# Two-layer cross-attention block: the feed-forward's short matmuls grouped by row shape, its neighbours taken two at a time, and the first group's keys made first

## The chip, the core and the metric

The kernel runs on one core of a Trainium2 chip. The metric is the time of one execution on the device, in microseconds (us), as the median of several runs. The kernel before takes 3205.06 us (3 runs, 3204.47 to 3205.57).

A core has a matmul engine (PE in the profile; its loading of the stationary operand is PEld), and three engines for elementwise work: VectorE (DVE), ScalarE (ACT) and GpSimd (POOL). SyncE (SP) issues most transfers. Each engine works through its own list of instructions in order; semaphores tie the lists together. Matmul results go to PSUM, 8 banks of 128 x 512 floats.

## What is computed

Two layers of the same block over `x` (4 x 512 x 320) with a context (4 x 1601 x 192): self-attention, cross-attention, feed-forward, all in float32. Cut to what matters here:

```python
def _attn(x, ctx, wq, wk, wv, wo, bo, heads):        # 20 heads of 16
    q, k, v = heads_of(x @ wq), heads_of(ctx @ wk), heads_of(ctx @ wv)
    a = softmax(einsum('bhid,bhjd->bhij', q, k) * 16 ** -0.5)
    return merged(einsum('bhij,bhjd->bhid', a, v)) @ wo + bo

h1 = _ln(x, n1_g, n1_b)
x = _attn(h1, h1, q1, k1, v1, o1_w, o1_b, heads) + x
h2 = _ln(x, n2_g, n2_b)
x = _attn(h2, context, q2, k2, v2, o2_w, o2_b, heads) + x
h3 = _ln(x, n3_g, n3_b)
proj = h3 @ ff_w1 + ff_b1                            # 320 -> 2560
a, g = split(proj, 2, axis=-1)
ff = a * gelu(g) @ ff_w2 + ff_b2                     # 1280 -> 320
return ff + x
```

## The kernel before

The work is a list of *units* in a fixed order. In each layer there are 20 units of self-attention (4 batch items, 5 groups of 4 heads), 20 of cross-attention and 4 of feed-forward (one for each batch item). `main` (L1065) runs an attention unit, `ff_main` (L1170) a feed-forward unit. The program is written out by hand in the order in which each engine is to work (a manual schedule), so what stands next to what on PE is decided while the kernel is built.

**Side work.** Everything that is not the core of a unit is put in *chains* of steps: layer norms (`turn`, L490: transposes into the tile `hps`, the matmuls of L497), query and key projections (`queries` L693 and `keys` L719: tiles `qps`, `kps`), values (`vps`), and the output projections after attention (`project` L1016: tile `ops`). The matmuls of the projections and of the values use 32 columns of the PE array at a time, four of them side by side; one step is 12 matmuls. A step has a cost (an estimate in the units of the planner, 0.95 for an output projection, 1.43 for queries or keys of self-attention) and a due round. `tick` adds to a credit in each round, enough for all steps to be done by when they are due, up to 4.0. `steps` (L398) takes steps off the chains as long as the credit allows: beside the feed-forward (`beside` true) a first step needs 0.5 of its cost in credit, and a second one right behind it 3.0 of its cost; `steps(False)` takes a step only at a credit of 3.0.

**Feed-forward.** The 320 rows of `ff_w1` are cut into two slices of 128 rows and a rest of 64 rows. The tile `w1r` holds the rest for the `a` half of the columns on partitions 0 to 63 and for the `g` half on partitions 64 to 127; `hT[:, 2]` holds the last 64 rows of the input twice, to match. A chunk `c` is 128 of the 1280 hidden columns; there are 10. For each chunk `full` (L1192) makes the four matmuls of 128 rows (two slices for `a`, two for `g`; L1194) and `rest` (L1203) the two of 64 rows, which use the two halves of the array at the same time (L1206). `gate` (L1210) then computes gelu on ACT and the product on DVE (L1213), which gives the tile `hid` (some chunks lie in the `kT` buffer). Chunks go in pairs. In float32 one matmul of the program is two in the profile: the eight matmuls of a pair's `full` are x16, its four of `rest` x8. After the ten chunks come four products with `ff_w2` (tile `yps`, L1233, 40 matmuls in all) and the addition to `x`. `beside` (L1173) is called before the first and before the second chunk of a pair and after each `yps`: it lets `give` put in rounds of the next attention unit's score maxima (tile `sps`, L903) and calls `steps`.

**PSUM.** `ps_st` has 4 tiles of one bank, `ps_m` 2 tiles of two banks. A pair of chunks takes two of the first kind for `a` and one of the second for `g`. A step beside the feed-forward takes a tile of `ps_st`, a round of maxima one of `ps_m` and two of `ps_st`. A tile is free again when its last reader (for `a` the product on DVE) is done.

**The start.** The first layer norm is followed by queries and keys of units 0 and 1; `to_slots` (L632) moves those of unit 0 out of PSUM in four pieces each, alternately on ACT and DVE (L643, L641). Then come four rounds of unit 0's score maxima (`sps`, reduced on DVE, L919), with a step of values between two rounds; `max_end` (L963) writes the maxima into the query tile by eight small transfers, two of them on POOL's queue, after which the first scores (`st`, L1074) may start. While `start["on"]` is set, steps take `ps_m` tiles once the rounds have begun.

Of the kernel before, what the change touches and what calls it, by code (L numbers as in the profile page):

```python
# [9 lines left out]
F32 = mybir.dt.float32  # L10
# [9 lines left out]
FF = 4 * D  # L20
L = 2
EPS = 1e-5
P = 128
# [20 lines left out]
NHC = FF // P  # L44
# [4 lines left out]
FK = [(0, 0, P), (1, P, P)]  # L49
REST = D - 2 * P  # L50
# [16 lines left out]
def kernel(ctx: ExitStack, tc: tile.TileContext, x, context, ws, out):  # L67
# [18 lines left out]
    nc = tc.nc  # L86
# [9 lines left out]
    ps_st = ctx.enter_context(tc.tile_pool(name="ps_st", bufs=4, space=PSUM))  # L96
    ps_m = ctx.enter_context(tc.tile_pool(name="ps_m", bufs=2, space=PSUM))
# [8 lines left out]
    for b in range(2):  # L106
        k, o = (const.tile([P, 1], F32, name=f"{n}{b}") for n in ("keep", "ones"))
# [11 lines left out]
    for i in range(2):  # L119
        m = const.tile([P, SLOT], F32, name=f"nmax{i}")  # L120
# [26 lines left out]
    for b in range(2):  # L147
        k = const.tile([P, 1], F32, name=f"kept{b}")
# [5 lines left out]
    for b in range(2):  # L154
        rows = slice(b * GD, (b + 1) * GD)
# [20 lines left out]
    w1 = wpool.tile([P, 2, 2 * FF], F32, name="w1")  # L176
# [6 lines left out]
    w1r = wpool.tile([P, FF], F32, name="w1r")  # L183
# [121 lines left out]
    at = 0  # L305
# [23 lines left out]
    chains = {n: deque() for n in ("divide", "project", "slots", "norm", "context", "early", "proj", "values")}  # L329
# [6 lines left out]
    start = {"on": True, "both": False}  # L336

    def step_bank(shape, name):

        if start["on"] and start["both"]:  # L340
            return ps_m.tile([P, 2, 512], F32, tag="m", name=name)[:, 0]
        return ps_st.tile(shape, F32, tag="st", name=name)

    def warm(n):

        ps = step_bank([P, 512], "wps")
        for _ in range(n):
            nc.tensor.matmul(ps[:, : 4 * P], lhsT=ident, rhs=fill, start=True, stop=True)
# [4 lines left out]
    def add(chain, cost, f, due, ready=yes, soon=yes):  # L353
        chains[chain].append((cost if isinstance(cost, tuple) else (cost,), due, ready, soon, f))
# [7 lines left out]
    def pick():  # L362
        heads = [
            (q[0][1] + late_by(n), n)
            for n, q in chains.items()
            if q and q[0][2]() and q[0][3]() and (q[0][0][0] != LIGHT or clock["lights"])
        ]
        return min(heads)[1] if heads else None

    def run(chain):  # L370
        costs, _, ready, _, f = chains[chain].popleft()
        assert ready(), chain
        f()
        clock["credit"] -= sum(costs)
# [19 lines left out]
    def tick():  # L394
        clock["round"] += 1
        clock["credit"] = max(-2.0, min(4.0, clock["credit"] + pace()))

    def steps(beside, lights=1):  # L398


        tick()
        clock["lights"], clock["slots"] = lights, 1
        clock["tiles"] = True if beside is None else None
        done = 0
        while True:
            name = pick()
            if name is None:
                break
            cost = sum(chains[name][0][0])
            if cost >= 0.1:  # L410
                share = (0.5, 3.0) if beside else (9.0, 9.0) if beside is False else (0.5, 0.75, 1.5)
                least = cost * share[done] if done < len(share) else 3.0
                if clock["credit"] < (3.0 if beside is False else least):
                    break
                done += 1
                if clock["tiles"] is not None:
                    clock["tiles"] = name in ALIKE
            run(name)
            if cost == LIGHT:
                clock["lights"] -= 1  # L420
            clock["slots"] -= name == "slots"
        clock["tiles"] = None

    def until(test, name):
        while not test():
            assert chains[name], name
            run(name)
# [221 lines left out]
    def add_proj(u):  # L649
        wq, wk = wq2 if u.cross else wq1, wk1  # L650
        chain = "early" if u.early else "proj"
# [13 lines left out]
        first = units[u.i - u.g]  # L665
# [125 lines left out]
        def add_queries():  # L791
            if u.g == 0 and u.cross:
                add(chain, 0.0, hold, due - 4, yes, lambda: "h" in u.own)
            for part in range(parts):
                add(chain, (0.05 + 0.427 / parts,) * 3, lambda part=part: queries(part), due - 2, unread)

        if not u.cross:
            add_queries()
            add(chain, (0.477,) * 3, keys, due, free)
        else:  # L800
            add(chain, 2.45, keys_of_context, keys_due, free)
            add_queries()
            for _ in range(HG):
                add(
                    "slots", 0.0, lambda: u.kslots and u.kslots.popleft()(), keys_due,
                    lambda: u.keyed, lambda: clock["slots"] > 0,
                )
# [251 lines left out]
    def round_of(scores, maxima):  # L1059

        then = [f() for f in scores] + [f() for f in maxima]
        for f in then:
            f()
# [106 lines left out]
    def ff_main(u, give, nxt):  # L1170
        done = 0

        def beside(room, n):  # L1173

            nonlocal done
            if room:
                for extra in give(done, True)[1]:
                    round_of([], extra)
            done += n
            if done == u.steps - 1 and nxt is not None and nxt.kind != "ff":  # L1180
                max_reduce(nxt)
                max_end(nxt)
            steps(True)
            for _ in range(n - 1):
                steps(False)

        hc = one.tile([P, 6, N], F32, tag="ctxT", name="hid")
        hid = [hc[:, i, :] for i in range(6)]

        hid += [kbuf[1][:, i * N : (i + 1) * N] for i in range(3)] + [kbuf[2][:, :N]]  # L1190

        def full(c, i, ps):  # L1192
            for k, at, n in FK:
                nc.tensor.matmul(  # L1194
                    ps,
                    lhsT=w1[:, k, i * FF + c * P : i * FF + (c + 1) * P],
                    rhs=u.hT[:, k, :],
                    start=(k == 0),
                    stop=False,
                )  # L1200
            return ps

        def rest(c, pss):  # L1203
            for i, ps in enumerate(pss):
                rows = slice(i * REST, (i + 1) * REST)
                nc.tensor.matmul(  # L1206
                    ps, lhsT=w1r[rows, c * P : (c + 1) * P], rhs=u.hT[rows, 2, :], start=False, stop=True
                )

        def gate(c, pss):  # L1210
            gl = prs.tile([P, N], F32, tag="pr", name="gl")
            nc.scalar.activation(gl, pss[1], AF.Gelu, bias=b1[:, NHC + c : NHC + c + 1])  # L1212
            nc.vector.scalar_tensor_tensor(hid[c], pss[0], b1[:, c : c + 1], gl, ALU.add, ALU.mult)  # L1213

        for c in range(0, NHC, 2):

            beside(True, 2)
            gates = ps_m.tile([P, 2, 512], F32, tag="m", name="fps")
            pss = []
            for i in range(2):  # L1220
                if i:
                    beside(False, 2)
                ps = ps_st.tile([P, 512], F32, tag="st", name="fps")
                pss.append([full(c + i, 0, ps), full(c + i, 1, gates[:, i])])
            for i in range(2):
                rest(c + i, pss[i])
            for i in range(2):
                gate(c + i, pss[i])
        ff_read.append(u)
        for t in range(NQ):  # L1230
            ps = ps_st.tile([P, 512], F32, tag="st", name="yps")
            for c in range(NHC):
                nc.tensor.matmul(  # L1233
                    ps[:, :D],
                    lhsT=hid[c][:, t * P : (t + 1) * P],
                    rhs=w2[:, c, :],
                    start=(c == 0),
                    stop=(c == NHC - 1),
                )
            nc.vector.tensor_tensor(xs[u.b][:, t, :], ps[:, :D], xs[u.b][:, t, :], ALU.add)  # L1240
            if u.l == L - 1:
                dma(out=out[u.b, t * P : (t + 1) * P, :], in_=xs[u.b][:, t, :])
            beside(True, 1)
        after(u)
# [35 lines left out]
    def left(v):  # L1280
        return sum(map(len, v.pairs))
# [75 lines left out]

    add_norms(0)
    add_proj(units[0])
    warm(5)  # L1360
    add_proj(units[1])
    until(lambda: not chains["proj"], "proj")
    add_values(units[0])
    add_proj(units[2])
    first = units[0]
    first.pairs = max_pairs(first)
    start["both"] = True
    while left(first):
        round_of([], first.pairs[0].popleft() + first.pairs[1].popleft())
        if left(first):  # L1370
            run("values")

    run("proj")
    run("values")
# [8 lines left out]
    start["on"] = start["both"] = False  # L1383
    run("proj")

    for _ in range(3):
        run("values")
    clock["credit"] = 0.0

# [45 lines left out]
```

## Time and profile before

| | us |
|---|---|
| median of 3 runs | 3205.06 |
| the profiled execution | 3204.68 |
| its span (first to last instruction) | 3202.9 |
| PE busy in the span | 3167.7 |
| DVE / ACT / POOL busy | 2068.9 / 1972.4 / 1202.3 |
| feed-forward of layer 0: 1329.77 to 1633.00 | 303.23, PE busy 299.75 |
| feed-forward of layer 1: 2920.14 to 3202.90 | 282.76, PE busy 278.68 |
| the first 36 us | PE busy 29.75 |

The profile page has a line of busy time for each engine and, further down, groups of equal instructions. The timeline view lists instructions in order of time, merged where equal ones follow each other: start, length, engine, line, operation, output<-inputs, rows*columns of the PE array that a matmul uses, its size and how many (x); in square brackets the idle time before it and what ended it. As matmuls are pipelined and their ends are modelled, lengths overlap; the time that a group takes is read from its start to the start of the next. "The granted clock" is the share of its full clock that PE was given.

### The profile page before, as it was taken

The page shows a single profiled execution, that of the slowest core. Times are in us where ns is not written, and L with a number is a line of the kernel's source. Part 1 is how long each engine was busy: PE and PEld are TensorE (multiplying, and loading weights), DVE is VectorE, ACT ScalarE, POOL GpSimd, SP SyncE. Part 2 cuts the span into 40 slices and gives each one's busy share as a digit, 9 for nine tenths or more (in the row PEclk, how much of TensorE's full clock was granted, in tenths as well). Part 3 has the DMA queues.
Part 4 walks back from the last instruction along what each step waited for, and adds up shares of the span by engine and source line. Part 5 has one row for each costly group of instructions (what it writes and reads, how often), then busy time and mean ns, then how long its engine had stood idle before and what let it go on. Part 6 is the DMA issues. An engine that isn't in the chain of part 4 may idle for free. (4 is left out here: it accounts for less than half of the span.)

```text
span 3202.9 us, 81370 instructions
## 1 busy us (share of the span) xinstructions
PE 3167.7 (99%) x33970; PEld 1462.6 (46%) x33970; DVE 2068.9 (65%) x2663; ACT 1972.4 (62%) x3951; POOL 1202.3 (38%) x1617
## 2 busy tenths in 40 slices
PE   8999999999999999999999999999999999999999
PEld 3444444444444444354444444444444444443555
DVE  7787778778678677422247777777777777773221
ACT  4666577777777777611146665778778777785110
POOL 5555334443443443201125553344444444432000
PEclk9999999999999999999999999999999999999999
DMA  2220011100100100100012100110010010001000
GB/s 66 56 70 17 14 27 38 33 21 20 32 21 21 31 16 11 39 6 0 1 30 61 34 14 14 24 27 16 16 32 9 16 32 11 14 10 37 9 11 15
DMA packets 104851, 77.84 MB, mean 24 GB/s; under 512 B 42908, under 2 KB 95012, under 8 KB 104484
## 3 DMA queue, kind: packets, MB, share of 16 engines
q1 hardware_dynamic: 104400, 72.63, 9.2%
q8 instruction: 268, 4.39, 0.6%
q14 instruction: 99, 0.81, 0.1%
q0 software_dynamic: 64, 0.00, 0.0%
q10 hardware_dynamic: 20, 0.00, 0.0%
HBM read 33.04 MB, written 7.93 MB: 13 GB/s over the span
## 5 line engine op out<-in xcount | busy, mean ns | idle before, releaser
L1080 ACT ACTIVATE pr<-st 128x512 f32<-128x512 f32 (+1 forms) x2720 | 1408.8, 602 | 430.1 <-PE sps L903 366.4
L1074 PE MATMUL st<-q,kT 32*128 32x512 f32 (+1 forms) x5440 | 1363.3, 614 | 3.8 <-DVE nmax L919 1.5
L919 DVE TENSOR_REDUCE pm<-sps 128x2 f32<-128x1024 f32 (+1 forms) x974 | 1133.9, 1203 | 269.0 <-PE sps L903 262.7
L903 PE MATMUL sps<-kT,q 32*128 32x512 f32 x5120 | 1273.6, 620 | 14.3 <-DVE nmax L919 11.3
L1111 POOL TENSOR_TENSOR o<-o,vo 128x512 f32<-128x512 f32 x576 | 734.3, 1275 | 1373.1 <-ACT vo L1110 1201.8
L1074 PEld LDWEIGHTS st<-q,kT 32*128 32x128 f32 (+1 forms) x5440 | 504.0, 181 | 520.0 <-ACT pr L1080 291.7
L1094 PE MATMUL av<-pr,vals 128*32 128x512 f32 (+1 forms) x5440 | 729.3, 605 | 0.2
L919 DVE TENSOR_REDUCE nmax<-sps 128x2 f32<-128x1024 f32 (+1 forms) x339 | 378.2, 1156 | 148.0 <-PE sps L903 145.9
L903 PEld LDWEIGHTS sps<-kT,q 32*128 32x128 f32 x5120 | 405.3, 183 | 125.9 <-issue 81.4
L1110 ACT COPY vo<-av 128x512 f32<-128x512 f32 x576 | 339.7, 590 | 45.5 <-PE av L1094 41.4
L1094 PEld LDWEIGHTS av<-pr,vals 128*32 128x32 f32 (+1 forms) x5440 | 110.0, 108 | 493.3 <-ACT pr L1080 480.1
L1194 PE MATMUL fps<-hT,w 128*128 128x512 f32 x640 | 288.2, 599 | 1.9 <-DVE hid L1213 1.9
L1212 ACT ACTIVATE gl<-fps,b 128x512 f32<-128x512 f32 x80 | 50.7, 684 | 386.7 <-PE fps L1206 386.7
L647 POOL TENSOR_SCALAR q<-qst,keep,zero 64x128 f32<-64x128 f32 (+1 forms) x476 | 231.1, 486 | 59.9 <-ACT qst L711 26.7
L1194 PEld LDWEIGHTS fps<-hT,w 128*128 128x128 f32 x640 | 117.4, 190 | 148.8 <-issue 142.4
L438 POOL TENSOR_SCALAR root<-root 128x4 f32<-128x4 f32 x23 | 5.3, 231 | 332.7 <-DVE root L432 332.2
L1213 DVE SCALAR_TENSOR_TENSOR hid<-fps,b,gl 128x512 f32<-128x512 f32 x48 | 33.8, 746 | 147.5 <-ACT gl L1212 147.5
L1021 PEld LDWEIGHTS ops<-wo,aT 112*32 112x32 f32 (+1 forms) x3072 | 97.8, 110 | 68.3 <-issue 37.1
L699 PE MATMUL qps<-hT,wq 112*32 112x128 f32 (+3 forms) x2880 | 125.5, 308 | 0.5 <-DVE pm L919 0.5
L1021 PE MATMUL ops<-wo,aT 112*32 112x160 f32 (+1 forms) x3072 | 125.2, 300 | 0.2
L699 PEld LDWEIGHTS qps<-hT,wq 112*32 112x32 f32 (+1 forms) x2880 | 86.3, 110 | 79.1 <-issue 38.9
L1240 DVE TENSOR_TENSOR x<-yps,x 128x320 f32<-128x320 f32 x32 | 15.7, 491 | 146.5 <-PE yps L1233 146.5
(88 smaller groups left out, 2259.6 us busy)
## 6 DMA issues: line engine op xcount, KB each, us to landing
kT<-kst SPq DMA_DIRECT2D x320, 48.0 KB
aT<-o SPq DMA_DIRECT2D x320, 32.0 KB
q<-turned SPq DMA_DIRECT2D x636, 1.0 KB
w<-in_L_xattn_ff_w_dram SPq DMA_DIRECT2D x20, 256.0 KB
ctxT<-ctxT SPq DMA_DIRECT2D x24, 208.0 KB
ctxT<-ctxT SPq DMA_DIRECT2D x12, 416.0 KB
ctxin<-in_ctx_dram SPq DMA_DIRECT2D x24, 192.0 KB
w<-in_L_xattn_ff_w_dram SPq DMA_DIRECT2D x20, 160.0 KB
```

Source lines behind the costliest of these rows:

```text
L647: nc.gpsimd.tensor_scalar(to, stage[rows, :w], keep[b][rows], more[rows], ALU.mult, ALU.add)
L699: nc.tensor.matmul(ps[to, :w], lhsT=wq[:n, k, gs], rhs=first.hT[:n, k, at[i] : at[i] + w], start=(k == 0), stop=(k == 2),)
L903: nc.tensor.matmul(ps, lhsT=u.q[j * SLOT : (j + 1) * SLOT, t * P : (t + 1) * P], rhs=u.kT[j * SLOT : (j + 1) * SLOT, u.k0 + s * 512 : u.k0 ...
L919: nc.vector.tensor_reduce(to[:, j : j + n], part, AX.X, ALU.max, negate=(ns == 1))
L1021: nc.tensor.matmul(ps[f : f + m, : D // 2], lhsT=aT[:n, k, t * P + f : t * P + f + m], rhs=wo[:n, k, cols], start=(k == 0), stop=(k == 2),)
L1074: nc.tensor.matmul(st[:r, :], lhsT=u.kT[rows, u.k0 + u.cols[c] : u.k0 + u.cols[c] + r], rhs=u.q[rows, :], start=True, stop=True)
L1080: nc.scalar.activation(p[:r], st[:r], AF.Exp)
L1094: nc.tensor.matmul(ps[i * SLOT : (i + 1) * SLOT, :], lhsT=columns_of[:r, head : head + SLOT], rhs=pr.pop((c, j))[:r, :], start=True, stop= ...
L1110: nc.scalar.copy(vo, ps)
L1111: nc.gpsimd.tensor_tensor(u.o, u.o, vo, ALU.add)
L1194: nc.tensor.matmul(ps, lhsT=w1[:, k, i * FF + c * P : i * FF + (c + 1) * P], rhs=u.hT[:, k, :], start=(k == 0), stop=False,)
L1212: nc.scalar.activation(gl, pss[1], AF.Gelu, bias=b1[:, NHC + c : NHC + c + 1])
```

## The change

Four edits. In `ff_main` the rests of two successive pairs are made in one block: the rests of pair c close its accumulation, and right behind them the rests of pair c+2 open theirs, in newly taken PSUM tiles; the slices of 128 rows of pair c+2 follow later and close it. With five pairs, blocks stand after pairs 0, 4 and 8 (the last one alone). In `steps` the thresholds beside the feed-forward become 2.2 and 1.1 of the step's cost: a first step waits until the credit is enough for two. In `add_proj` the keys of unit 0 come before its queries. At the start the first unit's projections are run before the second's are added, the steps between the four rounds are a projection, a projection, values, and the next in turn, and four further steps of values (in place of three) are run behind the first group.

```diff
-                share = (0.5, 3.0) if beside else (9.0, 9.0) if beside is False else (0.5, 0.75, 1.5)
+                share = (2.2, 1.1) if beside else (9.0, 9.0) if beside is False else (0.5, 0.75, 1.5)
...
         if not u.cross:
-            add_queries()
+            if u.i:
+                add_queries()
             add(chain, (0.477,) * 3, keys, due, free)
+            if not u.i:
+                add_queries()
...
-        def rest(c, pss):
+        def full(c, pss, ahead):
+
             for i, ps in enumerate(pss):
-                rows = slice(i * REST, (i + 1) * REST)
-                nc.tensor.matmul(
-                    ps, lhsT=w1r[rows, c * P : (c + 1) * P], rhs=u.hT[rows, 2, :], start=False, stop=True
-                )
+                for k, at, n in FK:
+                    nc.tensor.matmul(
+                        ps,
+                        lhsT=w1[:, k, i * FF + c * P : i * FF + (c + 1) * P],
+                        rhs=u.hT[:, k, :],
+                        start=ahead and k == 0,
+                        stop=not ahead and k == 1,
+                    )
+
+        def rests(c, pss, ahead):
+
+            for e in range(2):
+                for i, ps in enumerate(pss[e]):
+                    rows = slice(i * REST, (i + 1) * REST)
+                    nc.tensor.matmul(
+                        ps,
+                        lhsT=w1r[rows, (c + e) * P : (c + e + 1) * P],
+                        rhs=u.hT[rows, 2, :],
+                        start=ahead,
+                        stop=not ahead,
+                    )
...
+        def banks():
+            gates = ps_m.tile([P, 2, 512], F32, tag="m", name="fps")
+            return [[ps_st.tile([P, 512], F32, tag="st", name="fps"), gates[:, e]] for e in range(2)]
+
+
+        pss = None
         for c in range(0, NHC, 2):
-
-            beside(True, 2)
-            gates = ps_m.tile([P, 2, 512], F32, tag="m", name="fps")
-            pss = []
-            for i in range(2):
-                if i:
-                    beside(False, 2)
-                ps = ps_st.tile([P, 512], F32, tag="st", name="fps")
-                pss.append([full(c + i, 0, ps), full(c + i, 1, gates[:, i])])
-            for i in range(2):
-                rest(c + i, pss[i])
-            for i in range(2):
-                gate(c + i, pss[i])
+            ahead = pss is not None
+            if not ahead:
+                beside(True, 2)
+                pss = banks()
+
+            for e in range(2):
+                if e or ahead:
+                    beside(ahead and not e, 2)
+                full(c + e, pss[e], not ahead)
+            these, pss = pss, None
+            if not ahead:
+                rests(c, these, False)
+                if c + 2 < NHC:
+                    pss = banks()
+                    rests(c + 2, pss, True)
+            for e in range(2):
+                gate(c + e, these[e])
...
     warm(5)
+    until(lambda: not chains["proj"], "proj")
     add_proj(units[1])
-    until(lambda: not chains["proj"], "proj")
     add_values(units[0])
...
-    while left(first):
+    for chain in ("proj", "proj", "values", None):
         round_of([], first.pairs[0].popleft() + first.pairs[1].popleft())
-        if left(first):
-            run("values")
+        if chain:
+            run(chain)
...
-    for _ in range(3):
+    for _ in range(4):
         run("values")
```

## The prediction

> **What bounds the kernel now.** I read the page's busy times first, then PE's timeline in the feed-forward, where the order changes most, then the list of waits, and last the start.
>
> ```profile
> span 3202.9 us, 81370 instructions
> PE 3167.7 (99%) x33970; PEld 1462.6 (46%) x33970; DVE 2068.9 (65%) x2663; ACT 1972.4 (62%) x3951; POOL 1202.3 (38%) x1617
> ```
>
> PE is busy 99% of the span, no other engine over 65%. So time is won only where PE gets shorter, or in the 35 us (3202.9 - 3167.7) in which it waits. The change leaves the number and kinds of matmuls as they are (17,133 in both programs), so PE gets shorter only through their order. What order costs is seen in the last feed-forward, where nothing stands between the chunks (PE's timeline):
>
> ```profile
> 3132.85 7.03 PE L1194 MATMUL fps<-hT,w 128*128 128x512 f32 x16
> 3139.81 1.99 PE L1206 MATMUL fps<-hT,w1r 64*128 64x512 f32 x8
> 3141.73 7.13 PE L1194 MATMUL fps<-hT,w 128*128 128x512 f32 x16
> 3148.79 1.99 PE L1206 MATMUL fps<-hT,w1r 64*128 64x512 f32 x8
> 3150.71 7.13 PE L1194 MATMUL fps<-hT,w 128*128 128x512 f32 x16
> ```
>
> Read from start to start: the slices take 6.96 us behind a product of the same 128*128 shape (3132.85 to 3139.81) and 7.06 behind the 64*128 rests (3141.73 to 3148.79); the rests take 1.92 (3139.81 to 3141.73). How much of that is matmul is shown by the weight loads inside one block of rests:
>
> ```profile
> 3166.86 0.19 PEld L1206 LDWEIGHTS fps<-hT,w1r 64*128 64x128 f32 x2
> 3167.29 0.19 PEld L1206 LDWEIGHTS fps<-hT,w1r 64*128 64x128 f32 x2 [0.24 <-issue]
> ```
>
> They advance by 0.43, for two matmuls side by side. Four such steps make 1.72 of the 1.92, and sixteen steps of 0.43 make 6.87 of the slices' 7.06. So a block costs 0.20 over its matmuls each time PE's shape changes into it and out of it: 0.20 for rests, 0.19 to 0.20 for 128*128.
>
> **The cost of a step beside the feed-forward** (PE's timeline at two places):
>
> ```profile
> 1407.38 1.02 PE L1021 MATMUL ops<-wo,aT 112*32 112x160 f32 x24
> 1408.34 3.70 PE L1194 MATMUL fps<-hT,w 128*128 128x512 f32 x8
> ...
> 255.77 2.64 PE L1021 MATMUL ops<-wo,aT 112*32 112x160 f32 x72
> 258.34 0.70 PE L1074 MATMUL st<-q,kT 32*128 32x512 f32 x2
> ```
>
> One step alone takes 0.96. Three in a row take 2.57 (255.77 to 258.34), two take 1.75 (161.75 to 163.50 in the same view), so a further one adds 0.82: a block of steps has 0.14 of its own.
>
> **Part 1, fewer changes of shape.** I counted the blocks of one shape in the order in which each kernel issues its matmuls, in the eight feed-forwards. Rests: 40 blocks before, 24 after (24 rather than 20, since pair 8 has a block alone). Blocks of 128*128 entered from another shape: 56 before, 44 after. Blocks of 32-column steps: 25 before, 17 after (the 16 output projections stood alone; now twelve of them stand in six blocks x48). Maxima: as many as before. So 16 x 0.20 + 12 x 0.20 + 8 x 0.14 = 3.2 + 2.4 + 1.1 = 6.7 us less. Bounds: all 36 at the cheapest price (0.14) 5.0, all at the dearest (0.20) 7.2. Outside the feed-forward the count goes from 1735 to 1737, as layer norms behind the first one fall otherwise: +0.3, bounds 0 and 0.8.
>
> That a block of eight rests runs on at 0.43 is not shown as such. The nearest row is inside the block of four: its second pair uses the same halves of the array as the first, with other weights and banks, and follows 0.43 later. I take that.
>
> [...] The row above decides: loads for the same halves start while the matmul before still runs.
>
> **Part 2, waits for PSUM in the feed-forward.** Two kinds stand in PE's timeline:
>
> ```profile
> 1358.82 1.09 PE L497 MATMUL hps<-ident,hn 128*128 128x128 f32 x8
> 1360.55 3.70 PE L1194 MATMUL fps<-hT,w 128*128 128x512 f32 x8 [0.64 <-DVE hid L1213]
> ...
> 1558.24 1.14 PE L903 MATMUL sps<-kT,q 32*128 32x512 f32 x8
> 1559.91 1.50 PE L725 MATMUL kps<-hT,wk 112*32 112x256 f32 x24 [0.53 <-DVE hid L1213]
> ```
>
> Behind the rests, two transposes or a round of maxima take the two free one-bank tiles, and the next matmul waits for the first product on DVE. The transposes took 1.73, 1.67 and 1.73 where two between products take 0.87: 2.5 us lost in three places. The four rounds of maxima took 1.67 where one at the start takes 1.07 (19.87 to 20.94): 2.4 lost. Together 4.9. The rests of the first began at 1356.91, and the tile came free at 1360.5, 3.6 later: gelu starts 2.1 after, takes two times 0.68, and each product 0.75; the second tile is free 4.3 after. After the change the doubled block lasts 0.10 + 8 x 0.43 + 0.10 = 3.6, so a first tile is free when the step behind it starts, a second one 0.7 later. Two transposes there wait 0.2 (2 places). Maxima, which need both, wait 0.6 (2 places); behind one of these a values step must wait until DVE has reduced the maxima (1.2 and 0.6, from 1560.43): 1.4. Two rounds of maxima stand behind a pair of slices and ahead of the next pair's tiles and lose 0.6 each, as now. Sum 0.4 + 1.2 + 1.4 + 1.2 = 4.2, so 0.7 less than now. Bounds: none wait (-4.9), or nine places wait 0.86 each (7.7, +2.8). Gates lie two at a time as before; their ACT and DVE work is hidden behind slices (6.9 us a pair against 1.4 on each), and costs 1.4 a pair if that cover goes.
>
> **Part 3, the start** (PE, DVE and POOL timelines):
>
> ```profile
> 15.56 1.48 PE L725 MATMUL kps<-hT,wk 112*32 112x256 f32 x24
> 17.34 1.24 PE L903 MATMUL sps<-kT,q 32*128 32x512 f32 x8 [0.30 <-DVE kT L641]
> ...
> 33.86 0.70 PE L1074 MATMUL st<-q,kT 32*128 32x512 f32 x2 [1.52 <-issue]
> ```
>
> ```profile
> 15.56 0.54 DVE L641 TENSOR_SCALAR kT<-kps,keep,ones 64x256 f32<-64x256 f32 x1
> 16.73 0.55 DVE L641 TENSOR_SCALAR kT<-kps,keep,ones 64x256 f32<-64x256 f32 x1 [0.63 <-ACT kT L643]
> ```
>
> ```profile
> 27.99 2.48 POOL L647 TENSOR_SCALAR q<-qst,keep,zero 64x256 f32<-64x256 f32 x4 [5.04 <-ACT qst L711]
> 30.41 1.30 POOL L974 DMA_DIRECT2D q<-turned  x2
> ```
>
> The eight pieces of unit 0's queries and keys come out of PSUM one after another, alternately on ACT and DVE. The first round of maxima needs all keys, but only the first half of the queries. Now keys are last, so it waits for the eighth piece (16.73 + 0.55) and starts at 17.34. With keys first it waits for the sixth (15.56 + 0.54 = 16.10) and starts at 16.17: 1.17 earlier. Unit 1's projections move from ahead of the rounds into them. The rounds follow each other every 2.46 (19.87, 22.33, 24.78), set by DVE's reductions (9.79 / 4 = 2.45); a round and a projection on PE take 1.07 + 1.39 (24.78 to 27.24) = 2.46, so they just fit; if not, each of two adds some 0.1. Behind the rounds, unit 2's queries go to POOL (27.99), POOL's transfers follow at 30.41, and `st` at 33.86; POOL had been idle for 5.04, so all of this moves by the same 1.17. SP's loads are all issued by 10.6 us; the keys' weights, used at 12.96 without a wait, are now wanted at 11.60, and the last of them lands by 10.5. PE has less to do ahead of `st`, one values step, which goes into a wait of 0.5 a round for DVE; uncovered it costs 1.11 (37.51 to 38.62). Sum -1.2, bounds -1.2 and 0.
>
> **Sum.** -6.7 + 0.3 - 0.7 - 1.2 = -8.3 against the profiled execution's 3204.68 (span 3202.9 and 1.8 around it): 3196.4. The median of the runs is 0.38 above that execution, so 3196.8. All bounds together reach from 3205.06 - 13.3 = 3191.8 to 3205.06 - 1.4 = 3203.7.
>
> **Rivals.** (a) Only the shapes count, start and waits give nothing: -6.7 + 0.3 = -6.4, 3198.7. For it: a wait that goes often comes back one step later. Against: the start's chain has idle engines all along. 0.12. (b) All waits in the feed-forward go too: 3196.8 - 4.2 = 3192.6. For it: tiles are taken one chunk earlier, out of the steps' way. Against: maxima still need three tiles. 0.08. (c) Layer 0's share is lost again in layer 1's first units, where PE waits for the maxima on DVE (0.34 to 0.54 at 1633.19, 1638.74, 1647.16 and 1679.59): its part of the 6.7 is 8 x 0.20 + 4 x 0.20 + 5 x 0.14 = 3.1, so 3199.9. Against: DVE is busy 79.14 of that feed-forward's 303.23 us, so it has no work left over that would not move along. 0.06. (d) Slower: the rests taken ahead hold two one-bank tiles and a two-bank one for a further chunk, and PE stands at each of the 16 doubled blocks until a tile is read out. It decides from (8.3 + 6.4) / 16 = 0.92 a block; at 1.2 the time is 3196.8 + 19.2 = 3216.0. For it: `hps` above waits 0.86 for one tile too few. Against: the tiles that a doubled block takes were last used by a step that ran a whole chunk (3.4 us) or more before. 0.04. (e) The order does not become what it says: no change, 3205.1. The counts of blocks speak against it. 0.02. The forecast has 0.68.
>
> **The numbers.** 0.2% of 3205 is 6.4 us, about what a measurement of this kernel can tell from no change: faster means below 3198.65. The forecast, (b) and two thirds of (a) are faster: 0.84. The rest of (a), (c) and (e) are the same: 0.12. Slower: 0.04. The range takes in (a) to (c) and leaves out the ends where all bounds meet: 3192.5 to 3200.8.
>
> **What would show it.** In the timeline of the last feed-forward: rests x16 of 3.63 from start to start, between x16 slices; x48 projections of 1.77. Feed-forward of layer 0 about 300 us (-3.1, its waits as now), of layer 1 about 278.5 (-3.6 and -0.7). `sps` first at 16.2, `st` first at 32.7. Wrong is what I say if rests x16 take 3.84 or more (joints cost as changes do), if `fps` or steps behind doubled blocks show waits over 0.9, or if `st` still starts near 33.9.

## The result, and the profile after

| | before | after |
|---|---|---|
| median of the runs, us | 3205.22 (8 runs, 3204.47 to 3210.42) | 3196.45 (8 runs, 3194.21 to 3199.00) |
| the profiled execution, us | 3204.68 | 3197.12 |
| its span | 3202.9 | 3195.3 |

The ratio is 0.9969, with a 95% interval of 0.996 to 0.9978: 0.3% faster, at 3196.45 against 3196.8 predicted. The page of the changed kernel:

```profile
span 3195.3 us, 81370 instructions
PE 3163.1 (99%) x33970; PEld 1466.6 (46%) x33970; DVE 2069.2 (65%) x2662; ACT 1972.4 (62%) x3951; POOL 1204.1 (38%) x1617
```

PE is busy 4.6 us less (3167.7 to 3163.1) with the same number of matmuls, and waits 3.0 us less. PE's timeline in the last feed-forward, where before there were blocks of 1.92:

```profile
3126.09 7.03 PE L1199 MATMUL fps<-hT,w 128*128 128x512 f32 x16
3133.05 3.70 PE L1212 MATMUL fps<-hT,w1r 64*128 64x512 f32 x16
3136.69 14.00 PE L1199 MATMUL fps<-hT,w 128*128 128x512 f32 x32
3150.62 3.70 PE L1212 MATMUL fps<-hT,w1r 64*128 64x512 f32 x16
3154.25 6.28 PE L1199 MATMUL fps<-hT,w 128*128 128x512 f32 x14
```

A block of eight rests takes 3.63 from start to start (3133.05 to 3136.69, 3150.62 to 3154.25), where two blocks of four took 3.84. The weight loads at the joint of two pairs' rests show why:

```profile
3151.58 0.19 PEld L1212 LDWEIGHTS fps<-hT,w1r 64*128 64x128 f32 x2 [0.23 <-issue]
3152.01 0.19 PEld L1212 LDWEIGHTS fps<-hT,w1r 64*128 64x128 f32 x2 [0.23 <-issue]
3152.44 0.19 PEld L1212 LDWEIGHTS fps<-hT,w1r 64*128 64x128 f32 x2 [0.23 <-issue]
```

They run through at 0.43, with no step at the joint. The steps two at a time (PE's timeline) take 1.77, as expected:

```profile
1403.72 1.84 PE L1024 MATMUL ops<-wo,aT 112*32 112x160 f32 x48
1405.49 3.70 PE L1199 MATMUL fps<-hT,w 128*128 128x512 f32 x8
```

At the start something stands that no part of the prediction has (PE's timeline):

```profile
16.16 1.14 PE L906 MATMUL sps<-kT,q 32*128 32x512 f32 x8 [1.72 <-DVE q L641]
17.23 2.79 PE L699 MATMUL qps<-hT,wq 112*32 112x256 f32 x24
19.95 1.44 PE L906 MATMUL sps<-kT,q 32*128 32x512 f32 x8
...
33.04 0.70 PE L1077 MATMUL st<-q,kT 32*128 32x512 f32 x2
```

The first round of maxima is at 16.16, 1.18 earlier, as predicted. But the projection behind it takes 2.72 instead of 1.39, and `st` at 33.04 is only 0.82 earlier. The view by stretches tells why (length; busy us and instructions of PE, PEld, DVE, ACT and POOL; PE's granted clock; DMA):

```profile
13.79:17.20 3.41, 1.69 (x21) 0.44 (x12) 2.09 (x4) 1.69 (x3) 2.69 (x4) 1.00 0.05 14
17.20:20.61 3.41, 3.41 (x32) 1.51 (x32) 2.51 (x4) 0.39 (x1) 0.66 (x2) 0.50 0.02 5
20.61:24.02 3.41, 3.41 (x48) 1.19 (x44) 2.51 (x4) 0.37 (x1) 2.77 (x6) 1.00 0.00 0
...
798.85:802.26 3.41, 1.85 (x48) 1.32 (x52) 2.70 (x4) 0.75 (x2) 1.26 (x1) 1.00 0.18 43
802.26:805.68 3.42, 3.42 (x71) 2.45 (x56) 0.40 (x1) 0.55 (x2) 0.00 (x0) 0.50 0.00 0
...
1580.50:1583.92 3.42, 2.10 (x28) 0.96 (x29) 2.80 (x5) 0.00 (x0) 0.00 (x0) 1.00 0.00 0
1583.92:1587.33 3.41, 3.41 (x16) 1.49 (x9) 1.12 (x4) 0.27 (x1) 0.00 (x0) 0.50 0.02 5
```

Three times PE runs at half its clock for 3.41 us, each time behind 3.41 us in which it was busy for only 1.69, 1.85 and 2.10. The kernel before has the fall at 802 alone, apart from one in its last 1.2 us. The one at 1583.9 stands in the feed-forward of layer 0 (PE's timeline):

```profile
1576.67 3.70 PE L1212 MATMUL fps<-hT,w1r 64*128 64x512 f32 x16
1580.31 1.73 PE L906 MATMUL sps<-kT,q 32*128 32x512 f32 x8
1583.36 1.04 PE L833 MATMUL vps<-wv,hT 112*32 112x128 f32 x24 [1.32 <-DVE nmax L922]
1584.33 6.03 PE L1199 MATMUL fps<-hT,w 128*128 128x512 f32 x10
```

Here maxima stand behind a doubled block and a values step behind them; the step waits 1.32 for DVE, as the prediction has it (1.4), and the slices that follow run at half clock, which it does not have.

Cut at the same instructions in both traces, the 7.6 us (3202.9 - 3195.3) come from these stages. The last column is the difference to before in experiments whose profile has no fall of the clock in that stage (in the second row, where before has one, to e11, which is the kernel before without it):

| stage | predicted | after | without a fall (from which run) |
|---|---|---|---|
| up to the division that ends unit 0 (64.9 us) | -1.2 | -0.19 | -1.78 (e7, e10) |
| on to the feed-forward of layer 0 | 0 | +0.25 (both have the fall at 802) | 0.05 (e10 against e11) |
| feed-forward of layer 0 | -3.1 | -1.55 | -3.20 (e4, e9) |
| the 84 us behind it | +0.3 | -2.27 | -2.27 (after itself) |
| on to the feed-forward of layer 1 | 0 | +0.36 | 0.01 (e9, e10) |
| feed-forward of layer 1 | -4.3 | -4.14 | -4.14 (after itself) |
| sum | -8.3 | -7.6 | -11.3 |

### The profile page after: what moved, and what is told of

It reads as the page before. It is cut to its first block, busy times and chain, and to the rows that moved or that the text cites. A ratio compares the mean times of both kernels' runs of the same rounds, so it can differ in the third digit from the quotient of the medians.

```text
span 3195.3 us, 81370 instructions
## 1 busy us (share of the span) xinstructions
PE 3163.1 (99%) x33970; PEld 1466.6 (46%) x33970; DVE 2069.2 (65%) x2662; ACT 1972.4 (62%) x3951; POOL 1204.1 (38%) x1617
## 3 DMA queue, kind: packets, MB, share of 16 engines
HBM read 33.04 MB, written 7.93 MB: 13 GB/s over the span
```

## The experiments

Each kernel stands on 5 to 11 runs, beside runs of the kernel before.

**The parts alone: e1 to e4.** e1 has only the blocks of rests (`full`, `rests`, `banks` and the loop), e2 only the line of thresholds, e3 only the start with the order of keys and queries, e4 all but e3's part:

```diff
 e2:
-                share = (0.5, 3.0) if beside else (9.0, 9.0) if beside is False else (0.5, 0.75, 1.5)
+                share = (2.2, 1.1) if beside else (9.0, 9.0) if beside is False else (0.5, 0.75, 1.5)
```

> The doubled blocks of rests alone; thresholds of steps and start as before. Theory A (each change of shape in the feed-forward costs 0.14 to 0.20 us): blocks of rests 40 to 24, blocks of 128*128 entered from another shape 56 to 47, steps as before: 16 x 0.20 + 9 x 0.20 = 5.0 us less, within 1.5 for waits in the feed-forward: 3200.2 against 3205.2. Theory B (the gain of the whole change lies mostly in the steps that stand two at a time and in what follows from them behind the first feed-forward): about 2 us less or none. The first 65 us and the stretch from 1629 to 1690 us as before.

> The thresholds of steps alone; rests and start as before. Prediction's own count: blocks of steps in the feed-forward 25 to 17, 128*128 and rests as before: 8 x 0.14 = 1.1 us less, and 0 to 0.8 given back outside it, so about -0.8. Theory C (the 2.2 us won behind the first feed-forward, between 1629 and 1690 us in the changed kernel, come with the steps: layer norms fall later there and a round of maxima that stood alone at 1679.59 us stands beside scores): -1.1 - 2.2 = -3.3, and that stretch is 2.2 us shorter though nothing else of the change is in it.

> The start alone; feed-forward and steps as before. Prediction: the first scores 1.2 us earlier and all that follows: -1.2. Theory D (read from the changed kernel's trace): the first round of maxima starts at 16.16, but the wait ahead of it lets the granted clock fall to 0.50 from 17.20 to 20.61 us, and the values step between the rounds of unit 2 costs 0.6: the first unit ends 0.2 us earlier, and the time is -0.2, within 0.5.

> Rests and steps together, start as before. If the three parts simply add: the whole change less the start. Theory A and C: 36 changes of shape less in the feed-forward (-6.7) and -2.2 behind the first one, less 1.5 lost to waits and to the clock in the first feed-forward: about -7.4 to -8.7. If the start carries 1.2 us as predicted, the time is 1.2 us above the changed kernel's; by theory D it is within 0.5 of it.

| | median (runs), us | ratio to before, 95% | feed-forward layer 0 | the 84 us behind it | feed-forward layer 1 |
|---|---|---|---|---|---|
| e1, rests | 3202.15 (11) | 0.9989 [0.998, 0.9998] | +0.79, with a fall | 0.0 | -3.41 |
| e2, steps | 3202.70 (11) | 0.9993 [0.9984, 1.0002] | -1.13 | -2.27 | -0.39 |
| e3, start | 3204.66 (11) | 0.9994 [0.9986, 1.0003] | 0.0 | 0.0 | +0.01 |
| e4, rests and steps | 3197.05 (11) | 0.9976 [0.9968, 0.9985] | -3.20 | -2.27 | -4.14 |

The three columns on the right are differences of the profiled executions to before. In the last feed-forward, with nothing between the chunks, the rests bring 3.41, the steps 0.39 and both 4.14. The 2.27 behind the feed-forward of layer 0 come with the steps alone, and are -2.20 to -2.29 in the profiles of all nine kernels that have them. The medians do not add up (against before's 3204.74: 2.6 and 2.0 alone, 7.7 together). A small part of that lies in the feed-forward itself (in layer 1, where no fall stands, 3.41 and 0.39 alone and 4.14 together). The clock has a share too, as e1 and e2 each show three falls in their profiles, e4 four, before one; how large it is in the medians is not shown. What the start brings could not be told from nothing: e3's profile is 1.00 ahead at the first round, falls to half clock at 17.0 and has lost all of it by the end of unit 0.

**The start and the feed-forward's rounds: e5 to e7.** e5 fills the wait ahead of the first maxima with two matmuls of 128 x 128 x 512, e6 runs besides one more values step behind the first group, e7 moves the rounds of maxima in the feed-forward by one chunk:

```diff
 e5:
     until(lambda: not chains["proj"], "proj")
+    warm(2)
 e6, besides:
-    for _ in range(4):
+    for _ in range(5):
         run("values")
 e7, on the changed kernel:
-                    beside(ahead and not e, 2)
+                    beside(ahead and bool(e), 2)
```

> The changed kernel with two more matmuls of 128x512 (on the identity, result unused) between the first unit's queries and the first round of maxima, where PE waited from 14.3 to 16.16 us. Theory D (the wait of 1.7 us lets the granted clock fall to 0.50 for 3.41 us, from 17.20 on): with PE busy there the clock stays at 1.00, the first projection between the rounds takes 1.4 us in place of 2.72, the first scores start at about 32.6 in place of 33.04, and the time is 0.4 us less. Rival: the slow projection comes from a wait for a tile or for weights; then it takes 2.7 as before, or the matmuls added delay the rounds and the time is the same or 0.3 more.

> As the kernel with two more matmuls at the start, and five steps of values in place of four ahead of the first scores, so that none stands between unit 2's rounds of maxima. Theory D: that step cost 0.6 to 0.8 us between the rounds (sps to st took 4.13 us there in place of 3.31); ahead of the scores it fits into their wait, so the first unit ends 1.0 to 1.2 us earlier than in the kernel before, and the time is 0.8 to 1.0 us under the changed kernel's. Rival (the step is hidden wherever it stands, as predicted): no difference to the kernel with two more matmuls alone.

> The changed kernel, but where the rests were taken ahead the rounds of maxima come before the second chunk of the pair, not right behind the doubled block. Theory E (in the first feed-forward a round behind a doubled block waits for the two products, and the step behind it for DVE's reductions: 1.98 us over its own time at 1580.31, and the clock falls to 0.50 for 3.41 us, another 1.5): no round stands there, the feed-forward of layer 0 is some 2 us shorter (a projection behind a round now waits up to 1.9), and the clock stays at 1.00 in it. Rival (rounds wait for tiles wherever they stand): the same within 0.7, with the waits at other places.

The medians are 3195.60 (5 runs, ratio 0.9966 [0.9953, 0.9978]), 3196.59 (7, 0.9971 [0.996, 0.9982]) and 3196.47 (5, 0.9969 [0.9956, 0.9981]); none differs from the changed kernel's by more than the intervals. The profiles tell more than the medians. e7, whose start is the changed kernel's to the instruction, shows the same wait of 1.71 us ahead of 16.16 and no fall behind it: `st` is at 31.48, and the end of unit 0 is 1.78 earlier than before. So the fall at 17.2 is not bound to the wait, and e5's clean start (`st` at 32.01) proves nothing for its two matmuls, which moreover put off the first round by 0.53. e6 has falls at 48.5 (two windows long), 802.8, 1041.8 and 1587.9; what its fifth values step is worth can't be read under them. e7 has falls at 800.7 and at 1561.9, where maxima and a keys step now stand together: the round that was moved made the same wait elsewhere (1.91 us at 1560.96).

**Where the clock falls.** In all nine traces of that time each fall begins a whole multiple of 3.4133 us after the others of its execution (in before 802.163 and, in the last microseconds, 3201.733, which is 703.0 such windows later; in the changed kernel 17.20, 802.26 and 1583.92, which are 230.0 and 229.0 windows apart), and where this grid lies differs from execution to execution. For each window the share of the array that its matmuls used can be added up: rows x columns x streamed columns of each, against 128 x 128 x 512 in 0.435 us (sixteen of them take 6.96 above; 128*128 is the largest shape in the traces and is taken as the whole array). In these nine traces the 23 falls stand behind windows with a share of 0.363 or less, and the 8296 windows without a fall behind them have more than 0.37. PE's busy time alone doesn't order them: e6 falls behind a window at 45.1 in which PE idled for 0.79 (share 0.36), and before does not behind one at 1037.7 with 1.69 idle (share 0.46). In e6's window PE is busy for 2.63 us, but with maxima and scores alone, each on 32*128 and so on a quarter of 128*128, and they make up only 1.23 us of the whole array. How often a spot is hit is estimated by the share of the grid's places at which a window falls under 0.368. For before that makes 0.35 at 46, 0.62 at 797 and 0.58 at 1035; for the changed kernel 0.40 at 13 to 15, 0.63 at 797, 0.58 at 1035 and 0.79 at 1580. Where the trace itself has a fall, the time at half clock lowers the windows that reach into it, so such an estimate is somewhat high: e7, with the same start and no fall there, gives 0.22. Four more kernels tested this.

**e8, e9 and e11.** Filling the two waits for `ctxT` that both kernels have, with matmuls that are thrown away:

```diff
 e8 on the changed kernel, e11 on the kernel before:
             pss, singles, both = quarter_banks("kps")
+            if u.l == 0 and u.g == 0 and u.b > 1:
+                for a in range(4):
+                    nc.tensor.matmul(pss[a][:P, :P], lhsT=ident[:P, :P], rhs=ident[:P, :], start=True, stop=True)
 e9 on the changed kernel:
+                    nc.tensor.matmul(pss[a][:SLOT, :P], lhsT=ident[:SLOT, :SLOT], rhs=ident[:SLOT, :], start=True, stop=True)
```

> The changed kernel with four more matmuls of 128 x 128 x 128 (0.87 us together, thrown away) ahead of the context keys of batch items 2 and 3 in layer 0, where PE otherwise waits 1.55 us (at 799.7) and 1.75 us (at 1037.8) for ctxT. In the nine traces so far all falls of the clock begin on one grid of 3.413 us whose place differs from execution to execution, and follow a grid window in which matmuls used less than 0.37 of the array (rows x columns x steps; 23 falls, all at 0.363 or less; 8296 windows without one, all at 0.372 or more). Theory F (use of the array in the window decides): the lowest use of any 3.413 us around 799 and 1036 goes from 0.26 and 0.20 to some 0.5 and 0.45, so no fall begins at 795 to 807 or 1033 to 1047 whatever the grid's place. By the changed kernel's trace these two places were hit with a chance of 0.63 and 0.58, at 1.6 us each: 1.9 us less on average, median about 3194.5. Rival G (falls are chance or heat, not use): falls there as before, 3196.5.

> As the one before, with the same four matmuls on 32 x 32 of the array in place of 128 x 128: PE is as long busy in the wait, but only a sixteenth of the array is used. Theory F (use of the array): the windows' use stays about 0.27 and 0.22, falls come at 802 and 1040 as in the changed kernel, median 3196.5 (3195.5 to 3197.5), and the profile shows a fall at one of the two places with a chance of about 0.85. Rival H (PE's idle time in the window decides): as good as the 128 x 128 ones, no fall at either, 3194.5.

> The kernel before with the same four 128 x 128 matmuls at its two ctxT waits (797.3 to 799.4 and 1035.4 to 1037.3 are the window starts with a use under 0.37 in its trace: chance 0.62 and 0.58; a third place, 46.1 to 47.3, 0.35, stays). Theory F: 1.9 us less on average, 3203.2, no fall at 802 or 1040. Rival G: 3205.1. If theory F holds for both kernels, the two changes without disturbed clocks differ by the sum of the undisturbed stage differences, about 11 us.

e8 takes 3193.19 (5 runs, 3191.78 to 3195.02; ratio 0.9956 [0.9942, 0.9969]), e9 3196.61 (5 runs, 3193.58 to 3196.83; 0.9967 [0.9954, 0.9979]), as the share of the array would have it; by PE's idle time they would be equal. Four of e9's five runs lie above all of e8's. Their profiles happen to have the grid in the same place, to 0.1 us. e8 by PE's timeline and by stretches (columns as above):

```profile
799.70 0.94 PE L752 MATMUL kps<-ident 128*128 128x128 f32 x6 [0.37 <-DVE pm L925]
800.56 3.07 PE L758 MATMUL kps<-ctxT,w 32*64 32x224 f32 x96
```

```profile
797.98:801.40 3.42, 3.05 (x35) 1.62 (x35) 3.41 (x6) 1.41 (x4) 1.26 (x1) 1.00 0.14 31
801.40:804.81 3.41, 3.41 (x106) 2.75 (x94) 0.62 (x1) 0.68 (x3) 0.00 (x0) 1.00 0.05 12
```

and e9 in the same views:

```profile
799.70 0.84 PE L752 MATMUL kps<-ident 32*32 32x128 f32 x6 [0.31 <-DVE pm L925]
800.47 4.86 PE L758 MATMUL kps<-ctxT,w 32*64 32x224 f32 x96
```

```profile
797.98:801.40 3.42, 3.04 (x34) 1.32 (x34) 3.41 (x6) 1.42 (x4) 1.26 (x1) 1.00 0.14 31
801.40:804.81 3.41, 3.41 (x87) 2.98 (x78) 0.00 (x0) 0.00 (x0) 0.00 (x0) 0.50 0.05 13
```

PE is busy 3.05 and 3.04 us of the window; the share of the array is 0.53 in e8 and 0.28 in e9; the clock stays at 1.00 in e8 and falls to 0.50 in e9, where the context keys then take 4.78 (800.47 to 805.25) instead of 3.00. e9 falls at 1040.3 too, e8 at neither place. e11 takes 3203.00 (11 runs; ratio 0.9993 [0.9984, 1.0001]), 3203.2 being expected. Seven of its runs lie between 3202.66 and 3203.02, the others up to 3206.68, as the places at 31 (where `st` waits longer than in before) and 47 us stay open; that interval alone would not show a gain, but its profile has no fall at 802 or 1040, and the mean granted clock is 1.000 in those seven runs and 0.999 in the other four.

**e10, cover everywhere.** e8's matmuls, one `warm` in the wait at the start, and in the feed-forward a step ahead of the maxima:

```diff
     until(lambda: not chains["proj"], "proj")
+    warm(1)
...
         def beside(room, n):
 
             nonlocal done
+            steps(True)
             if room:
                 for extra in give(done, True)[1]:
                     round_of([], extra)
...
-            steps(True)
             for _ in range(n - 1):
```

> The changed kernel with cover at all the places where its windows can fall under 0.37: the four 128 x 128 matmuls at both ctxT waits, one of 128 x 128 x 512 in the 1.7 us wait ahead of the first maxima, and in the feed-forward a step taken ahead of a round of maxima rather than behind it, so that the values step behind the fourth doubled block does not wait 1.3 us for DVE. Theory F: no fall of the clock at all up to the last microseconds, 2.46 expected falls x 1.6 = 3.9 us less, and 1.0 less for the wait: 3191.5 (3190 to 3193.5), with first st at about 31.5 and the feed-forward of layer 0 at -4 against the kernel before; the runs agree within 1.5 us. Rival G: one to three falls, 3195.5.

It takes 3190.52 us (5 runs, 3190.16 to 3190.72; ratio 0.9949 [0.9937, 0.9962]): faster than both kernels, with runs that differ by 0.56 where the changed kernel's differ by 4.79, and no fall of the clock up to 3189. Its start (PE's timeline):

```profile
14.39 1.12 PE L348 MATMUL wps<-q,ident 128*128 128x512 f32 x2
16.17 1.14 PE L909 MATMUL sps<-kT,q 32*128 32x512 f32 x8 [0.65 <-DVE q L641]
17.24 1.50 PE L699 MATMUL qps<-hT,wq 112*32 112x256 f32 x24
18.70 1.14 PE L909 MATMUL sps<-kT,q 32*128 32x512 f32 x8
...
31.49 0.70 PE L1080 MATMUL st<-q,kT 32*128 32x512 f32 x2
```

The projection between two rounds takes 1.46, not 2.72, the rounds come every 2.5, and `st` stands at 31.49 with no wait. And the place in the feed-forward of layer 0 that had the wait of 1.32 (the same view):

```profile
1573.17 3.70 PE L1215 MATMUL fps<-hT,w1r 64*128 64x512 f32 x16
1576.80 0.86 PE L836 MATMUL vps<-wv,hT 112*32 112x128 f32 x24
1577.60 1.58 PE L909 MATMUL sps<-kT,q 32*128 32x512 f32 x8
1579.10 7.13 PE L1202 MATMUL fps<-hT,w 128*128 128x512 f32 x16
```

From the block of rests to the slices there are now 2.30 us of steps and maxima (1576.80 to 1579.10), where the changed kernel has 4.02 (1580.31 to 1584.33). That feed-forward is 4.74 shorter than before's, 1.54 more than the 3.20 that it gains without a fall alone.

## Why the prediction was right

**Shapes: right in mechanism and size.** A block of eight rests takes 3.63, as worked out; the bet that the joint runs on at 0.43 held. Two steps in a row take 1.77, as said. The last feed-forward came out at -4.14 where -4.3 was said (3.6 for shapes and 0.7 for waits), that of layer 0 at -3.20 without a fall where -3.1 was said.

**Waits in the feed-forward: right in size, not in what they trigger.** In the changed kernel's layer 0, two rounds behind doubled blocks take 1.66 instead of 1.07 (0.6 each said), the values step waits 1.32 (1.4 said), two pairs of slices wait 0.49 each (0.6 each said) and the transposes behind a block take 1.15 instead of 0.87 (0.2 said). My sign of an error, a wait over 0.9 behind a doubled block, contradicts my own sum, which had 1.4 there. What failed is that a wait was priced at its length: with 3.0 us of maxima, a wait and a narrow step the window's use was 0.34, and the next 3.41 us ran at a clock of 0.50, 1.65 more (-1.55 against -3.20).

**The start: right at the first round, wrong behind it, twice.** The chain that I gave for the first round stands as described: `sps` 1.18 earlier. "All of this moves by the same 1.17" held for POOL's transfers where no fall stands (issued at 30.41 before, 29.28 in e10), but not for `st`, which moved by 2.37 in e10 and 2.38 in e7. The wait of 1.52 in before ends with the landing of the first of these transfers: it lands at 33.77, 3.36 after its issue, and `st` starts at 33.86. I took that stretch as fixed. The view of the tile `turned` (from 26 to 36 us in before, from 25 to 34 us in e10) gives for the two transfers:

```profile
DMA to landing us min/median/max: 2.8/3.1/3.4
DMA to landing us min/median/max: 1.8/1.9/2.1
```

In all five traces with the old start the first transfer takes 3.36 to 3.67, and `st` starts 0.09 after it has landed; in the eight with the new start it takes 1.79 to 1.81, and `st` follows PE's own work without a wait. Why it is faster is open: in those five a transfer of 16 KB on the DMA queue `instruction` starts at 31.5 to 31.8, while POOL's is under way, and in the eight none does, but no experiment shows that the one delays the other. Against the gain, the values step that "goes into a wait" or costs 1.11 was put ahead of a later round, and the stretch from `st` to the end of unit 0 is 0.6 longer. Net -1.78 against -1.2; with a fall, as the changed kernel's profile has it behind its new wait of 1.72, -0.19.

**Outside the feed-forward: the term was +0.3, and it measured -2.27.** I counted changes of shape there and did not follow the order. PE's timeline of before, some 50 us behind the feed-forward:

```profile
1678.46 0.59 PE L1074 MATMUL st<-q,kT 32*128 32x512 f32 x2
1679.59 1.14 PE L903 MATMUL sps<-kT,q 32*128 32x512 f32 x8 [0.54 <-DVE nmax L919]
1680.66 1.06 PE L1094 MATMUL av<-pr,vals 128*32 128x512 f32 x8
1681.55 0.84 PE L830 MATMUL vps<-wv,hT 112*32 112x128 f32 x24
1682.64 1.29 PE L1074 MATMUL st<-q,kT 32*128 32x512 f32 x3 [0.25 <-DVE nmax L919]
```

and of the changed kernel at the same place:

```profile
1679.47 0.70 PE L1077 MATMUL st<-q,kT 32*128 32x512 f32 x2
1679.48 0.70 PE L906 MATMUL sps<-kT,q 32*128 32x512 f32 x2
1680.00 0.59 PE L1077 MATMUL st<-q,kT 32*128 32x512 f32 x2
1680.01 1.01 PE L906 MATMUL sps<-kT,q 32*128 32x512 f32 x4
```

Before, a round of maxima stands alone and costs 1.07 and two waits, 0.54 and 0.25; after, the rounds here stand beside scores, at the same time (1679.47 and 1679.48). By these rows that is 1.86 of the 2.27. It comes with the thresholds (e2): what the steps have left in credit decides which layer norm and which round falls where. That was luck and not my working.

**So the total was right by luck: two misses cancel.** 2.6 us more behind the feed-forward of layer 0 and 0.6 at the start, against two falls of the clock more than before in the profiled execution (1.59 and 1.65). The measured interval is 3192.4 to 3198.2 (0.996 to 0.9978 of 3205.22). Of the rivals, (b), no waits left, at 3192.6 lies in it, but its condition did not come: the waits stayed. (a) and (c), at 3198.7 and 3199.9, lie outside. What (a) denies at the start is there where no fall stands (-1.78) and almost gone with one (-0.19), so the changed kernel's own profile would not have told it from the forecast on that point. (c) fails in its mechanism too: layer 0's share was not lost in layer 1 (+0.36 on the way, 0.01 without a fall). (d) did not come: no `fps` waits behind a doubled block.

## What to carry to other kernels

Group small matmuls by their shape on the array: each change cost 0.14 to 0.20 us here, and blocks of one shape may be joined across different outputs. A wait can cost more than its own length: here waits of 1.32 and 1.72 us among narrow matmuls stood ahead of falls of the clock that cost 1.65 and 1.59 besides, and with 128*128 matmuls in the two waits for `ctxT` (e8) the profile had no fall there, so such a wait is worth filling with full-width work or moving away from narrow steps. Where runs of one kernel differ by steps of some 1.6 us, as those of e3 and e11 do, look at the granted clock before comparing parts. And a wait that ends with a small transfer is as long as the transfer takes, which here was 3.4 or 1.8 us for the same bytes: read it from the trace after the change, not only before.

## What the runs showed of the hardware

**In these traces the clock falls behind windows in which little of the array is used.** In all thirteen traces, up to 3180 us, there are 29 falls to 0.50. They begin on the execution's grid of 3.413 us and last one window or two. The windows ahead of them have a share of 0.383 or less; of some 12,000 windows at full clock without a fall behind them three have less than that (0.373 to 0.380), and the next is at 0.414. Idle time overlaps widely: PE idled for only 0.38 in e9's window ahead of 801.4, and for 1.75 in the changed kernel's window at 1037.8, share 0.43, which no fall follows. Rows alone or columns alone, counted in the same way, overlap too: in the changed kernel the windows ahead of the three falls have 0.58 to 0.74 by rows and 1.01 to 1.16 by columns (matmuls that run side by side are added up), and windows that no fall follows have 0.48 by rows (at 361.9) and 0.64 by columns (at 1327.9). The waits in those three windows are 1.72, 1.55 and 1.32 us long, but the idle time did not settle it: e9 kept PE busy for 3.04 of 3.42 us with a share of 0.28 and fell all the same, and e8, busy for 3.05 with a share of 0.53, did not.

**A fall of one window cost 1.59 and 1.65 us** in the two stages where it can be read: -0.19 against -1.78 at the start, -1.55 against -3.20 in the feed-forward. By an estimate from these traces, 3.41 us at a clock of 0.50 lose half of that, 1.71. That where the grid lies decides how many falls a run has would explain the spread of the runs: nine runs of e3 lie between 3204.57 and 3205.04 and two at 3202.93 and 3202.99, as one fall less would have it, and e10, in whose trace no window up to 3180 us is under 0.368, has a spread of 0.56.

What stays open: why POOL's first transfer takes 3.62 to 3.67 in e1, e2, e4 and e11 and 3.36 in the profiled execution of before, at an unchanged start (with a first round 0.2 later in three of them, that makes `st` 0.3 to 0.5 later), and how much of the 2.27 beyond the 1.86 belongs to the layer norms' new places.
